# The w_down product of a gated MLP by seven instead of eight block products, with sums on GpSimd and VectorE, the keys' norms by a DMA of diagonals, and six instead of eight tiles for x

## The chip, the cores and the metric

The kernel runs on one core of a Trainium2 chip. A core has TensorE (matrix products, results to PSUM), VectorE, ScalarE and GpSimd (elementwise work; GpSimd does not read PSUM in this kernel) and SyncE, whose queue issues nearly all DMAs here. In the profile they are PE, with PEld for the loads of stationary operands, DVE, ACT, POOL and SP. The metric is the time of one execution on the device in microseconds; less is better. Before the change: 2123.92 us, median of 3 runs (2123.28 to 2125.16).

## The reference

32 sequences of 512 positions and 256 features, all in float32. Each goes through a delta-rule attention, an MLP and a gated MLP, each with layer norms and a residual sum:

```python
def delta(x, ...):
    q, k, v = split(x @ gates_w + gates_b, 3)
    lr = x @ lr_w + lr_b
    k = k / norm(k)
    A = tril(k k^T, -1) + I
    u = solve_triangular(A, v, lower=True)
    y = (q k^T) @ (lr * u)
    return y @ out_w + out_b

h = layernorm(x)
h = h + delta(layernorm(h) * dn_g + dn_b, ...)
h = h + relu((layernorm(h) * mn_g + mn_b) @ w1 + b1) @ w2 + b2
x = x + h
f = layernorm(x)
x = x + (silu(f @ wg.T) * (f @ wu.T)) @ wd.T   # wg, wu, wd: integers / 127; 768 hidden features
```

The last product of the last line is the one the change rewrites: for each sequence, a 512x768 matrix of hidden values times 768x256.

## The kernel before

Sequences are worked on in 16 pairs (`NS = 2`), one after another in a software pipeline written out by hand. In the loop at the end of the kernel, pass g handles three pairs together: `new` (keys, Gram matrix, triangular solve), `old` (MLP, gate and up products) and `older` (w_down product and output). In passes 2 to 15, that is 14 times, all three exist. The order of instructions on TensorE, VectorE, ScalarE and SP is the order of the code (`manual_schedule`); only GpSimd's order is chosen by the framework when the kernel is built, from which operations it expects to be ready.

A pass with all three pairs runs so:

1. `gram_phase`: Gram blocks of the new keys. `give` (L543) writes the 32x32 diagonal blocks of each Gram matrix to DRAM (`given`).
2. `middle` (L921): for the two old sequences `mlp_in`, `mlp_out` and `normed`, with the w_down products of the two older ones between them. `downs` (L873) yields eight steps, one for each sequence and chunk of 128 positions; `more(k)` takes the next k. A step (`Project.step`, L752) multiplies the 128 positions by all of w_down: six calls of 128x256 summed in PSUM. After every second step VectorE adds the 512 columns into the residual `s.acc` (L770); after the fourth, one DMA of 512 KB writes the sequence out (L871).
3. `gated` (L844): for each of the six blocks of 128 hidden features a gate product, `silu` on ScalarE, an up product, and their product on VectorE (L863). The results are six tiles of tag `hid`, twelve buffers in all. Twelve steps run before the solve of the new pair begins, and the other twelve are interleaved with it (`solution`, `solve`, `merge`).
4. `values_phase`: the rest of the attention of the new pair, and keys of the `following` pair.

Two more chains run on the side, as generators that a `Side` object advances whenever code on TensorE calls `spend` with the number of columns it has just used. `norms` (L555) multiplies each diagonal Gram block by the identity and sums it on VectorE, eight operations, then takes the power -- with exponent 0.5 -- on GpSimd; it is spread over 4*1024 columns. `invert` (L575) fetches `given` as `blocks`, inverts 64 triangular 32x32 blocks at once in 31 steps on VectorE (L603 a product, L607 a sum), writes the result to DRAM as `found` and reads it back as `yb` and `yfull`; it is paced by `INVERT`, 22*1024 columns. `merge` (L626) puts the 32x32 inverses together to 128x128 ones; it begins with VectorE transposes of `yb` (L636 to L638) and a TensorE product of them (L644).

In PSUM there are two pools of four banks; `mlp_in`, `mlp_out`, w_down, gate and up share `ps_f`. A bank comes free for the fourth tile after it when the engine that read it is done.

The residual, `s.a`, stays in one of eight 512 KB tiles of tag `a` from the load of x to the output. `load_a(following)` stands in `middle` ahead of the last five w_down steps. In `fetch_residual` (L806) GpSimd adds b2 to a second copy of x (L809). In `Norm.measure` GpSimd takes the power r_f or r_m (L345) and a product mr_f or mr_m (L373), which ScalarE's `apply` (L376) waits for.

Of the kernel before, what the change touches and what calls it, by code (L numbers as in the profile page):

```python
# [14 lines left out]
P = 128  # L15
# [6 lines left out]
def kernel(  # L22
# [98 lines left out]
    def big(name):  # L121
        return wk.tile([P, NT, C], F32, tag="a", name=name, bufs=8)
# [59 lines left out]
    class Gates:  # L182
# [63 lines left out]

        def turned(self, lo_, name):

            dst = wk.tile([P, NF, C], F32, tag="hid", name=name, bufs=NS * NH)
# [42 lines left out]
        def load_rest(self):  # L292
            self.load(*CUTS[1])
            self.load(*CUTS[2])
            self.ow = wk.tile([P, NF, C], F32, tag="hid", name="ow", bufs=NS * NH)
# [7 lines left out]
    wdT = const.tile([P, NH, C], F32, name="wdT")  # L303

    class Dequant:
        def __init__(self, src, name, tag, bufs):
            rows, self.cols = src.shape
            self.name, self.parts = name, []
            k = 1024 // self.cols
# [12 lines left out]
        def turn(self, dst):  # L322
            for r0, m, wi in self.parts:
                wf = wi.bitcast(F32)
                nc.scalar.mul(wf, wi, WSCALE)
                for cc in range(self.cols // P):
                    pt = ps_f.tile([P, 512], F32, tag="mm", name=f"{self.name}_t{cc}_{r0}")
                    for r in range(m):
                        nc.tensor.transpose(pt[:, ts(r, P)], wf[:, r, ts(cc, P)], ident)
                    nc.scalar.copy(dst[:, cc, r0 * P : (r0 + m) * P], pt[:, : m * P])  # L330
                    yield

# [57 lines left out]
    def to_features(src, dst, tag):  # L390

        for f in range(NF):
# [3 lines left out]
            nc.scalar.copy(grouped(dst[:, f, :]), natural(pt))  # L396
# [37 lines left out]
    def normalized(s):  # L434
# [41 lines left out]
        s.ag = wk.tile([P, NF, T], F32, tag="feat", name=f"ag_{n}", bufs=4)  # L476
# [24 lines left out]
    def to_keys(s):  # L501
        to_features(s.a, s.ag, f"a{s.n}")

    def keys(s, o):
        n = s.n
        if o == 0:
            s.kT = wk.tile([P, NF, T], F32, tag="ka", name=f"kT_{n}")

            early = n // NS == 1
            s.aT = wk.tile(  # L510
                [P, NF, T], F32, tag="a" if early else "aT", name=f"aT_{n}", bufs=8 if early else 2
            )
# [6 lines left out]
        nc.scalar.copy(natural(s.kT[:, o, :]), grouped(pk))  # L519
        nc.scalar.copy(natural(s.aT[:, o, :]), grouped(s.ag[:, o, :]))  # L520
# [22 lines left out]
    def give(s, given):  # L543
# [5 lines left out]
        for i in range(NB):  # L549
            rows = slice(i * B, (i + 1) * B)  # L550
            nc.sync.dma_start(
                given[:, i].rearrange("b r c -> r b c"), s.gd[rows, :, rows]
            )

    def norms(g, seqs):  # L555
        ss = small.tile([P, NS, NT], F32, tag="ss", name=f"ss_{g}", bufs=2)
        for slot, s in enumerate(seqs):
            for j in range(NT):
                junk = wk.tile([P, C], F32, tag="junk", name=f"js_{s.n}_{j}", bufs=1)
                nc.vector.tensor_tensor_reduce(  # L560
                    out=junk[:, :P], in0=s.gd[:, j, :], in1=ident, scale=1.0, scalar=0.0,
                    op0=ALU.mult, op1=ALU.add, accum_out=ss[:, slot, j : j + 1],
                )
                yield
# [4 lines left out]
        yield  # L569
# [5 lines left out]
    def invert(g, given, seqs):  # L575
# [5 lines left out]
            given.rearrange("s b i r c -> (s b i) (r c)").unsqueeze(1).to_broadcast(  # L581
# [262 lines left out]
    def gated(seqs):  # L844

        for s in seqs:
            s.hid = []
            for o in range(NH):
                g = wk.tile([P, T], F32, tag="hid", name=f"hid_{s.n}_{o}", bufs=NS * NH)
                s.hid.append(g)  # L850
# [15 lines left out]
    def down(s, c):  # L866
        if c == 0:
            s.project = Project(ps_f, s.acc, s.hid, wdT, NH, f"f{s.n}")
        s.project.step(c)
        if c == NT - 1:  # L870
            nc.sync.dma_start(out[s.n].rearrange("(c p) d -> p c d", p=P), s.acc)  # L871

    def downs(seqs):  # L873

        for s in seqs:
            for c in range(NT):
                down(s, c)
                yield
# [27 lines left out]
    def new_given(g):  # L906
        return dram.tile([NS, NT, NB, B, B], F32, tag="given", name=f"given_{g}")
# [13 lines left out]
    def middle(old, older, following):  # L921

        one, two = old
        rest = downs(older) if older else iter(())
        more = lambda k: [next(rest, None) for _ in range(k)]
        mlp_in(one, 0)
        mlp_in(one, 1)
        more(1)
# [5 lines left out]
        more(1)  # L934
        mlp_out(two, 0)
        mlp_out(two, 1)
        more(1)
# [246 lines left out]
```

## Time and profile before

The profiled execution took 2119.41 us, of which the span of instructions is 2117.5 us; the granted TensorE clock was 0.994 of full.

| engine | busy, us | share |
|---|---|---|
| loads of stationary operands | 1365.6 | 64% |
| VectorE | 1257.1 | 59% |
| ScalarE | 666.7 | 31% |
| GpSimd | 307.3 | 15% |

One pass, from the first `pa` of `middle` at 1143.96 us; rows of the windows view, busy time in each stretch:

```profile
core 0: us, PE busy (x) PEld busy (x) DVE busy (x) ACT busy (x) POOL busy (x), PEclk, DMA share, GB/s
1143.96:1162.90 18.94, 18.94 (x74) 13.68 (x73) 10.46 (x38) 6.17 (x16) 3.27 (x3) 1.00 0.25 69
1162.90:1178.45 15.55, 15.55 (x73) 13.68 (x72) 13.54 (x48) 2.08 (x4) 1.21 (x2) 1.00 0.53 131
1178.45:1199.06 20.61, 20.61 (x50) 9.12 (x49) 12.42 (x30) 3.59 (x6) 0.00 (x0) 1.00 0.38 106
1199.06:1243.00 43.94, 43.50 (x194) 28.03 (x193) 26.68 (x93) 14.32 (x42) 7.06 (x21) 1.00 0.24 72
```

Each row is a stretch: its bounds and length, then for each engine the busy time and the number of instructions, the granted clock, and what the DMA engines did. The first stretch is `middle` up to the last `mlp_out`, the second the last six w_down steps, the third the first twelve steps of `gated`, the fourth the solve and what follows.

A row of a group of instructions, elsewhere in this document, reads: line, engine, operation, output<-inputs, shapes, count | total busy us, mean ns of one | idle time of the engine before them, and what it waited for. A call of a float32 matmul in the code appears as two MATMUL rows of half the work each (w_down: 32 x 4 x 6 = 768 calls, 1536 rows), each with its own load. Matmuls overlap, so the mean of one is longer than the distance between two.

### The profile page before, as it was taken

The page shows a single profiled execution, that of the slowest core. Times are in us where ns is not written, and L with a number is a line of the kernel's source. Part 1 is how long each engine was busy: PE and PEld are TensorE (multiplying, and loading weights), DVE is VectorE, ACT ScalarE, POOL GpSimd, SP SyncE. Part 2 cuts the span into 40 slices and gives each one's busy share as a digit, 9 for nine tenths or more (in the row PEclk, how much of TensorE's full clock was granted, in tenths as well). Part 3 has the DMA queues.
Part 4 walks back from the last instruction along what each step waited for, and adds up shares of the span by engine and source line. Part 5 has one row for each costly group of instructions (what it writes and reads, how often), then busy time and mean ns, then how long its engine had stood idle before and what let it go on. Part 6 is the DMA issues. An engine that isn't in the chain of part 4 may idle for free.

```text
span 2117.5 us, 24970 instructions
## 1 busy us (share of the span) xinstructions
PE 2062.4 (97%) x7982; PEld 1365.6 (64%) x7982; DVE 1257.1 (59%) x4122; ACT 666.7 (31%) x1659; POOL 307.3 (15%) x551
## 2 busy tenths in 40 slices
PE   5799999999999999999999999999999999999999
PEld 2575666757666675766757566675766757566675
DVE  3747575765756566475765756566475755656331
ACT  3433313333142332323323242332323323241230
POOL 3101202112020211102111020211102011020100
PEclk9799999999999999999999999999999999999999
DMA  4110332413333222332413233231332422233020
GB/s 132 38 33 8 112 88 60 123 33 99 84 90 107 63 78 63 112 87 67 125 36 94 77 98 102 61 90 50 112 87 70 122 52 88 68 102 85 14 60 20
DMA packets 232459, 163.67 MB, mean 77 GB/s; under 512 B 64993, under 2 KB 207976, under 8 KB 232328
## 3 DMA queue, kind: packets, MB, share of 16 engines
q1 hardware_dynamic: 229136, 160.23, 27.0%
q10 hardware_dynamic: 3112, 1.71, 0.3%
q8 instruction: 64, 1.05, 0.2%
q14 instruction: 67, 0.55, 0.1%
q0 software_dynamic: 80, 0.14, 0.0%
HBM read 95.95 MB, written 66.06 MB: 77 GB/s over the span
## 4 chain that ended last, share of the span: by engine, by line
PE 83%; DVE 10%; ACT 4%; issue 1%; DMA 1%; POOL 0%; ACTq 0%; DVEq 0%; SPq 0%
PE po_f L758 16%; PE pup L854 13%; PE pgate L854 11%; PE pg L533 6%; PE po_d L758 5%; PE pf L719 5%; PE pa L824 5%; PE po_m L758 5%; PE pk L515 5%; PE pm L719 3%; PE pz L719 3%; ACT a L454 2%; PE pr L698 2%; DVE bnst_a L339 2%; PE pu L708 2%
## 5 line engine op out<-in xcount | busy, mean ns | idle before, releaser
L854 PE MATMUL pgate<-hT_f,wgT 128*128 128x512 f32 x768 | 364.3, 597 | 2.0 <-ACT hid L861 1.5
L854 PE MATMUL pup<-hT_f,wuT 128*128 128x512 f32 x768 | 364.0, 596 | 0.0
L758 PE MATMUL po_f<-wdT,hid 128*128 128x256 f32 x1536 | 339.2, 379 | 0.0
L758 PEld LDWEIGHTS po_f<-wdT,hid 128*128 128x128 f32 x1536 | 291.8, 190 | 52.9 <-issue 14.8
L861 ACT ACTIVATE hid<-pgate 128x512 f32<-128x512 f32 x192 | 114.3, 596 | 620.8 <-PE pgate L854 620.8
L863 DVE TENSOR_TENSOR hid<-hid,pup 128x512 f32<-128x512 f32 x192 | 131.0, 683 | 253.8 <-PE pup L854 252.5
L854 PEld LDWEIGHTS pgate<-hT_f,wgT 128*128 128x128 f32 x768 | 143.1, 190 | 146.7 <-issue 135.1
L854 PEld LDWEIGHTS pup<-hT_f,wuT 128*128 128x128 f32 x768 | 143.4, 190 | 145.8 <-issue 129.9
L607 DVE TENSOR_REDUCE xc<-xt 128x8 f32<-128x16 f32 (+30 forms) x496 | 147.0, 296 | 17.1
L603 DVE TENSOR_TENSOR xt<-xc,blocks 128x16 f32<-128x16 f32 (+30 forms) x496 | 147.3, 297 | 11.5
L533 PE MATMUL pg<-kT 128*128 128x256 f32 (+3 forms) x512 | 142.0, 434 | 0.6 <-ACT kT L519 0.6
L533 PEld LDWEIGHTS pg<-kT 128*128 128x128 f32 x512 | 89.8, 190 | 58.9 <-issue 35.6
L515 PE MATMUL pk<-ag,wa 128*128 128x512 f32 x256 | 119.2, 600 | 1.5 <-ACT ag L396 1.5
L758 PE MATMUL po_d<-m,aT 128*128 128x256 f32 x512 | 116.1, 380 | 1.1 <-ACT m L741 1.0
L758 PE MATMUL po_m<-w2s,act 128*128 128x256 f32 x512 | 116.3, 379 | 0.3
L719 PE MATMUL pf<-a,dp 128*128 128x256 f32 x512 | 115.6, 379 | 0.0
L824 PE MATMUL pa<-hT_m,w1s 128*128 128x512 f32 x256 | 115.1, 592 | 0.0
L758 PEld LDWEIGHTS po_d<-m,aT 128*128 128x128 f32 x512 | 96.8, 190 | 21.4 <-issue 3.6
L719 PEld LDWEIGHTS pf<-a,dp 128*128 128x128 f32 x512 | 97.3, 190 | 19.6 <-issue 7.2
L758 PEld LDWEIGHTS po_m<-w2s,act 128*128 128x128 f32 x512 | 97.1, 190 | 15.0 <-ACT act L830 1.5
L830 ACT ACTIVATE act<-pa,b1s 128x256 f32<-128x256 f32 x128 | 53.8, 471 | 157.0 <-PE pa L824 157.0
L742 DVE TENSOR_TENSOR m<-pm,obrow 128x256 f32<-128x256 f32 x32 | 13.6, 425 | 146.1 <-ACT m L741 146.1
(167 smaller groups left out, 2624.1 us busy)
## 6 DMA issues: line engine op xcount, KB each, us to landing
a<-in_L_attn_x_dram SPq DMA_DIRECT2D x32, 512.0 KB, 4.9
x<-in_L_attn_x_dram SPq DMA_DIRECT2D x32, 512.0 KB, 4.6
out_dram<-a SPq DMA_DIRECT2D x32, 512.0 KB, 3.6
way_m<-turn_m SPq DMA_DIRECT2D x120, 128.0 KB, 2.3
hT_m<-way_m SPq DMA_DIRECT2D x30, 512.0 KB, 3.7
way_a<-turn_a SPq DMA_DIRECT2D x112, 128.0 KB, 2.5
ag<-way_a SPq DMA_DIRECT2D x28, 512.0 KB, 6.9
way_f<-turn_f SPq DMA_DIRECT2D x112, 128.0 KB, 2.4
```

Of the source, the lines that this page charges most:

```text
L339: nc.vector.bn_stats(st[:, c, :], src[:, c, :])
L515: nc.tensor.matmul(pk, lhsT=wa[:, f, ts(o, P)], rhs=s.ag[:, f, :], start=(f == 0), stop=(f == NF - 1),)
L533: nc.tensor.matmul(pg[:, :w], lhsT=s.kT[:, f, ts(j, P)], rhs=s.kT[:, f, j * P :], start=(f == 0), stop=(f == NF - 1),)
L603: nc.vector.tensor_tensor(t[:, :, : i + 1], xc[:, :, : i + 1], blocks[:, i, : i + 1].unsqueeze(1).to_broadcast([P, ncol, i + 1]), ALU.mult,)
L607: nc.vector.tensor_reduce(xc[:, :, i], t[:, :, : i + 1], axis=AX.X, op=ALU.add)
L719: nc.tensor.matmul(s.pp[:, o, :], lhsT=lhs[:, c, ts(o, P)], rhs=rhs[:, c, :], start=(c == 0), stop=(c == nk - 1),)
L758: nc.tensor.matmul(self.po[:, c % 2, :], lhsT=src[:, ts(c, P)], rhs=self.w[:, f, :], start=(f == 0), stop=(f == self.nk - 1),)
L824: nc.tensor.matmul(pa, lhsT=w1s[:, f, ts(o, P)], rhs=s.hT[:, f, :], start=(f == 0), stop=(f == NF - 1),)
L830: nc.scalar.activation(natural(s.act[:, o, :])[:, :, some], grouped(pa)[:, :, some], AF.Relu, bias=b1s[:, o : o + 1], scale=1.0,)
L854: nc.tensor.matmul(pp, lhsT=w[:, f, ts(o, P)], rhs=s.hT[:, f, :], start=(f == 0), stop=(f == NF - 1),)
L861: nc.scalar.activation(natural(g), grouped(pp), AF.Silu)
L863: nc.vector.tensor_tensor(natural(g), natural(g), grouped(pp), ALU.mult)
```

## The change

**w_down.** The 512 positions of a sequence become two halves. In a half the hidden values are a 2x2 arrangement of blocks, A[i,k]: i picks one of two chunks of 128 positions, k the even or the odd of the six blocks of 128 hidden features. w_down is arranged likewise: k, and one of two blocks of 128 outputs. A product of two such 2x2 arrangements takes eight block products, or seven with sums of blocks before and after (the Strassen-Winograd scheme). Each block product is three calls of 128x128, since k runs over three pairs of features. `Down.plain` makes three products of unchanged blocks, then has GpSimd overwrite the four A blocks with their combinations; `Down.combined` makes the other four and adds everything into the residual, on VectorE and GpSimd, and then writes the half out (256 KB). The combinations of w_down are made once, in `Combined`.

```diff
-    wdT = const.tile([P, NH, C], F32, name="wdT")
+    NP = NH // 2
+    wdS = const.tile([P, NP, 7, P], F32, name="wdS")
...
+            if cc == NH - 1:
+                b = lambda i: wdS[:, :, i, :]
+                minus = lambda o, x, y: nc.gpsimd.tensor_tensor(o, x, y, ALU.subtract)
+                minus(b(5), self.b12, b(0))
+                minus(b(3), b(6), b(5))
+                minus(b(4), b(6), self.b12)
+                minus(b(2), b(1), b(3))
...
+        def products(self, po, todo):
+            for i, (block, slot) in enumerate(todo):
+                for j in range(NP):
+                    nc.tensor.matmul(
+                        po[:, i, :], lhsT=self.A[block][:, j, :], rhs=wdS[:, j, slot, :],
+                        start=(j == 0), stop=(j == NP - 1),
+                    )
+                spend(NP * P)
+        def plain(self):
+            name = f"{self.s.n}_{self.half}"
+            po = ps_f.tile([P, 4, P], F32, tag="mm", name=f"po_x_{name}")
+            self.products(po, [((0, 0), 0), ((0, 1), 1), ((1, 1), 2)])
+            self.e = wk.tile([P, P], F32, tag="e", name=f"e_{name}", bufs=4)
+            nc.scalar.copy(self.e, po[:, 0, :])
+            first = self.acc[:, :, :P]
+            nc.vector.tensor_tensor(first, first, po[:, 1:3, :], ALU.add)
+            A = self.A
+            nc.gpsimd.tensor_tensor(A[1, 0], A[1, 0], A[1, 1], ALU.add)
+            nc.gpsimd.tensor_tensor(A[0, 0], A[1, 0], A[0, 0], ALU.subtract)
+            nc.gpsimd.tensor_tensor(A[0, 1], A[0, 1], A[0, 0], ALU.subtract)
+            nc.gpsimd.tensor_tensor(A[1, 1], A[1, 1], A[0, 0], ALU.subtract)
+        def combined(self):
+            name = f"{self.s.n}_{self.half}"
+            po = ps_f.tile([P, 4, P], F32, tag="mm", name=f"po_y_{name}")
+            self.products(po, [((0, 0), 3), ((1, 1), 4), ((1, 0), 5), ((0, 1), 6)])
+            w = wk.tile([P, 3, P], F32, tag="uv", name=f"uv_{name}", bufs=1)
+            acc, flat = self.acc, self.acc.rearrange("p c d -> p (c d)")
+            twice = lambda m: m.unsqueeze(1).to_broadcast([P, 2, P])
+            add = lambda o, x, y: nc.vector.tensor_tensor(o, x, y, ALU.add)
+            add(w[:, 0, :], self.e, po[:, 0, :])
+            add(w[:, 1:3, :], twice(w[:, 0, :]), twice(po[:, 1, :]))
+            add(acc[:, :, P:], acc[:, :, P:], twice(po[:, 2, :]))
+            add(acc[:, 0, P:], acc[:, 0, P:], po[:, 3, :])
+            nc.gpsimd.tensor_tensor(acc[:, 0, :P], acc[:, 0, :P], self.e, ALU.add)
+            nc.gpsimd.tensor_tensor(
+                flat[:, P:], flat[:, P:], w.rearrange("p b d -> p (b d)"), ALU.add
+            )
+            nc.sync.dma_start(
...
     def downs(seqs):
...
+        return [Down(s, h) for s in seqs for h in range(NT // 2)]
```

**The order in `middle`** (and likewise, in other places, in `last_middle` and after the last `gated`); the load of the following pair moves from here to the seventh step of `gated`:

```diff
         mlp_in(one, 1)
-        more(1)
+        for d in rest[:1]:
+            d.plain()
...
         normed(one, "f")
-        more(1)
+        for d in rest[1:2]:
+            d.plain()
         mlp_out(two, 0)
         mlp_out(two, 1)
-        more(1)
         turned(one, "f")
+        for d in rest[:1]:
+            d.combined()
         normed(two, "f")
-        if following:
-            for s in following:
-                load_a(s)
-        more(5)
+        for d in rest[2:]:
+            d.plain()
+        for d in rest[1:]:
+            d.combined()
```

**Norms.** The row of `given` is made 32 elements longer, so that a stride of 33 over it walks all diagonals; one DMA of 1024 single elements replaces the eight VectorE operations. The side chain is spread over 16*1024 columns.

```diff
-    def norms(g, seqs):
+    def norms(g, given, seqs):
         ss = small.tile([P, NS, NT], F32, tag="ss", name=f"ss_{g}", bufs=2)
-        for slot, s in enumerate(seqs):
-            for j in range(NT):
...
-                yield
+        nc.sync.dma_start(
+            ss.rearrange("p s t -> p (s t)"),
+            given.rearrange("s b i e -> (s b) (i e)")[:, :: B + 1].rearrange("q t -> t q"),
+        )
+        yield 4
...
-                kn_side = Side(norms(g, new), 10, 4 * 1024)
+                kn_side = Side(norms(g, given, new), 10, 16 * 1024)
```

**Room.** Tag `a` has six buffers instead of eight; `hid` becomes one tile of six blocks for each sequence, two buffers, which also hold weights at the start. For the first four sequences the keys' input is kept in natural order and one ScalarE copy for each half of the features goes away:

```diff
-        return wk.tile([P, NT, C], F32, tag="a", name=name, bufs=8)
+        return wk.tile([P, NT, C], F32, tag="a", name=name, bufs=6)
...
-        nc.scalar.copy(natural(s.kT[:, o, :]), grouped(pk))
-        nc.scalar.copy(natural(s.aT[:, o, :]), grouped(s.ag[:, o, :]))
+        if n >= 2 * NS:
+            nc.scalar.copy(natural(s.kT[:, o, :]), grouped(pk))
+            nc.scalar.copy(natural(s.aT[:, o, :]), grouped(s.ag[:, o, :]))
+        else:
+            nc.scalar.copy(s.kT[:, o, :], pk)
...
-            s.hid = []
+            s.hid = wk.tile([P, NH, T], F32, tag="hid", name=f"hid_{s.n}")
```

## Prediction

> **What bounds the kernel now.** I read the page's busy times first, then the chain that ended last, then the groups of instructions with shapes kept apart, then one steady stage in order of time, engine by engine.
>
> ```profile
> PE 2062.4 (97%) x7982; PEld 1365.6 (64%) x7982; DVE 1257.1 (59%) x4122; ACT 666.7 (31%) x1659; POOL 307.3 (15%) x551
> ...
> PE 83%; DVE 10%; ACT 4%; issue 1%; DMA 1%; POOL 0%; ACTq 0%; DVEq 0%; SPq 0%
> ...
> L758 PE MATMUL po_f<-wdT,hid 128*128 128x256 f32 x1536 | 339.2, 379 | 0.0
> ```
>
> TensorE is busy 97% of the span and is most of the chain; the w_down products are its third largest group. Shares over the span hide what happens within a stage, so here is one of the 14 stages that have a pair in the solve, a pair in the MLP and an older pair in w_down (TensorE, then VectorE and the DMA queue):
>
> ```profile
> 1143.96 3.60 PE L824 MATMUL pa<-hT_m,w1s 128*128 128x512 f32 x8
> ...
> 1162.91 15.70 PE L758 MATMUL po_f<-wdT,hid 128*128 128x256 f32 x72
> 1178.45 1.88 PE L854 MATMUL pgate<-hT_f,wgT 128*128 128x512 f32 x4
> ```
> ```profile
> 1155.52 0.35 DVE L589 RECIPROCAL di<-blocks 128x32 f32<-128x32 f32 x1
> ...
> 1175.38 0.29 DVE L603 TENSOR_TENSOR xt<-xc,blocks 128x136 f32<-128x136 f32 x1
> 1175.71 0.30 DVE L607 TENSOR_REDUCE xc<-xt 128x8 f32<-128x136 f32 x1
> ...
> 1190.08 0.42 DVE L607 TENSOR_REDUCE xc<-xt 128x8 f32<-128x256 f32 x1
> ```
> ```profile
> 1190.53 0.34 SPq L611 DMA_DIRECT2D found<-xc  x1
> 1192.25 0.91 SPq L618 DMA_DIRECT2D yb<-found  x2
> ```
>
> I count from 1143.96 as t=0. TensorE has no gap up to t=56. But from t=11.6 to t=46.5 VectorE is full too, but for some 2 us: the 31 steps of the inversion, a product and a sum each, fill the gaps between its other work and end at t=46.5. `found` and `yb` follow (issue at 48.3, 0.9 us, 2.0 us to landing: 4.6 us in all), and the merge, whose first transpose of `yb` ran at t=56.0, needs them. So there is a second chain, VectorE's, about 5 us behind the first. 59% busy does not show it.
>
> **The change, part by part.** *TensorE.* Each product of the code is two instructions (768 calls, 1536 rows). A stage has 96 of 128x256; 15.54 us for 72 in a row (the chain's piece) is 0.216 each: 20.7 us. It gets 2 sequences x 2 halves x 21 calls x 2 = 168 of 128x128. The nearest row is the last Gram block:
>
> ```profile
> 128.79 0.61 PE L533 MATMUL pg<-kT 128*128 128x128 f32 x4
> ```
>
> Its single duration is 274 ns, so (0.61-0.27)/3 = 0.113 from start to start; eight transposes of that width give (1.04-0.27)/7 = 0.110. 168 x 0.111 = 18.6 us: **2.1 us less a stage**, 34 us in all. A rule speaks against this: the Trainium skill, "TensorE: Matmul & The Clock Gate", § Back-to-back issue gap, says weight load and matmul together set the spacing of a narrow stream, and has 81 ns where its formula for the matmul alone has 56. That ratio on 0.111 makes 0.160: 27 us a stage, 6 us more instead of 2.1 less. The row is nearer: same type, same widths, a load per matmul (190 ns, overlapping the next). It runs in fours, though, and the new runs are 18 and 24 long; I take 0.111 and keep the rule as a rival.
>
> *GpSimd.* It gets 16 sums of 128x384 a stage, and 8 smaller ones into the output.
>
> ```profile
> L809 POOL TENSOR_TENSOR x<-x,b2s 128x1024 f32<-128x1024 f32 x32 | 74.7, 2356 | 34.3 <-DMA x<-in_L_attn_x_dram 32.3 <-PE pu L708 1.9
> ...
> L373 POOL TENSOR_TENSOR mr_m<-nmn_m,r_m 128x4 f32<-128x4 f32 x32 | 6.4, 200 | 2.5
> ```
>
> From these, 0.2 + 2.1 ns an element: 1.0 us for 384, 0.47 for 128. A dependent pair (r_m, then mr_m) has a gap of 0.08, so the four sums of a half take **4.2 us**. On average that hides. It doesn't where it bunches. In the new order the last three-product groups end at t=22.4 and 24.4, and their four-product groups are to start at 27.1 and 29.8. From 22.4 GpSimd has r_f and mr_f of the second sequence (1.3 us, released by VectorE about then), eight sums (8.5), and perhaps the two additions of the first group (1.4): the last sum is ready at 32.2 or 33.6. The last group wants it for its second product at 30.4. TensorE waits 1.8 to 3.2 us; bounds 0.5 (sums first, faster than the row) and 4. I take **2.6**.
>
> *VectorE.* A half had one 128x512 addition, 0.60 from start to start. It gets one of 256 columns after its first group and after the second 128, 256, 256, 128, two of them dependent. At about 1 ns a column (683 against 425 ns for 512 and 256) that is 0.36 + 1.38. Inside the full stretch fall three of the first kind and four of the second: 6.6 us for 2.4, **4.2 more**. It starts 1.2 us earlier (two groups of 2.6 us ahead of it become 2.0), and 1.0 us of waiting for ScalarE's `h_f` is filled. The inversion ends at 48.5 instead of 46.5. The norms' removal (8 rows of 0.37 us) frees time at t=-4 to 1, outside the stretch, where VectorE then idles until the first po_m at t=8: nothing.
>
> Then there is what the two engines share:
>
> ```profile
> 1156.11 1.23 DVE L592 TENSOR_TENSOR blocks<-blocks,ndi 128x1024 f32<-128x1024 f32 x1
> ```
> ```profile
> 1156.77 0.63 POOL L373 TENSOR_TENSOR mr_f<-nmn_f,r_f 128x4 f32<-128x4 f32 x1
> ```
> ```profile
> 1961.21 1.49 DVE L640 TENSOR_SCALAR rhs<-a,kn 128x256 f32<-128x256 f32 x1
> ```
>
> A 0.20 us GpSimd operation took 0.63 and ended 0.06 after VectorE's product of two SBUF operands. And a 0.35 us VectorE operation took 1.49 while a 2.35 us GpSimd addition ran beside it. The Trainium skill, "SBUF — State Buffer", § Who interferes with whom, makes it a rule: a VectorE instruction with two SBUF inputs and a GpSimd one that reads SBUF exclude each other, whole instruction against whole instruction. Every inversion step begins with such a product. But `xt` rows beside the short powers r_f kept their 250 ns, so the trace does not show this pair colliding. With the rule, some 8 steps among the sums lose 0.4 us each, 3.2 us (up to 6 with the additions): the inversion ends at 51.7; without it, at 48.5. The sums stream their operands as the 1024-wide addition does, so I go with the rule. At 51.7, `yb` lands at 56.3 and the merge's first product comes at 57.6 instead of 56.9; TensorE would have been there at 57.4 by the lines above, and the second sequence's transposes follow as late. Lateness also shows in PSUM: w_down, gate and up share four buffers, so the second `up` waits when the last group's four additions end over 5 us after its matmuls. For both I take **0.9 us**; bounds 0 and 2.7.
>
> *ScalarE* gets 4 copies of 128x128 a stage (266 ns); it is idle 9 us before the gates. *Norms by DMA*: one issue (about 0.5 us) ahead of `blocks` on SP, 1024 pieces of 4 bytes. Bounds for `blocks` 0.5 us (the issue) and 6 us (landing of b1s, 256 such pieces, in the crowded start); it lands near 8 and is wanted at 11, so 0; at worst 2.7 us of VectorE. The power waits for it on GpSimd with r_f behind, but is 6,554 columns late by its schedule, about 11 us. *Six tiles*: the next x can load only when an older output has left. On SP the outputs now wait for GpSimd's last addition (t≈42), with `hT_f` of the second sequence (wanted at t=55) and both loads behind: in by about t=52, wanted at 68. Free; without that cover each us late is one on the path.
>
> *Ends.* At the start ScalarE loses eight copies (620 ns) and VectorE 3 us of norms before the first inversion; TensorE waits there for both: -2. In the last middle, 10.4 us of products covering the m round trip become 6.7 and wait for sums: that eats its 2.1. The tail saves 2.1 and adds about 1.2 of small additions: -1.
>
> **Sum.** -2.1 + 2.6 + 0.9 = +1.4 a stage, x14 = +20, ends -3: span 2117.5 + 17 = 2134.5, execution 2119.41 + 17 = 2136. The median of the runs lies 4.5 above the profiled execution, so **2140**.
>
> **Rivals.** *The sums hide*: GpSimd takes eight sums before anything else and the exclusion hardly bites; -2.1 to -0.5, say -1.3 a stage: -18-3, 2103 (all of it kept: 2092). For it: POOL is idle 85% of the time, and its order is chosen by readiness, not by the code (the x addition ran after a later copy). Against: 8.5 us of dependent sums in 8 us. *Full exclusion*: 6 us on the inversion and 4 at the sums; +3.3, 2167. Slower, decided at t=46.5 to 49: once the last reduction ends beyond about 50 the merge moves out. *Narrow products pay for their loads*: 0.160 each, +6 a stage, 2220; against it the rows of 0.11. *A part that doesn't do what it says* (norms late, x late): 3 in 100.
>
> **Chances.** Mine 0.41 (own range 2122 to 2158), sums hide 0.38, full exclusion 0.15, loads 0.03, other 0.03. Range **2092 to 2172**: from the full saving to full exclusion. A difference of 0.2% (4 us) is what can be told from none. Of mine 0.06 and of the hidden sums 0.02 fall within it, and 0.01 of the rest: faster 0.37, same 0.09, slower 0.54.
>
> **What would show it.** The new products 0.111 apart, in runs of 18 and 24; sums of about 1.0 us; waits of the four-product groups on GpSimd, 2 to 3 us a stage; `xt` rows beside a sum longer than before; the last reduction at 50 to 53 after the first `pa`. I'm wrong if no product waits for GpSimd, if `xt` keeps its length, or if the spacing nears 0.16.

## The result and the profile after

The changed kernel takes **2115.79 us** (median of 6 runs, 2114.84 to 2116.86) against 2123.80 us (6 runs, 2123.28 to 2125.16): ratio 0.9961, 95% interval 0.9948 to 0.9974. It is faster by 0.4%; the prediction had 0.8% slower as the likeliest. The result lies inside its outer range (2092 to 2172), but not inside its own (2122 to 2158), and on the other side of the kernel before.

The profiled execution took 2116.25 us, its span 2114.5. First the page: busy times, chain of waits, groups.

```profile
PE 2037.7 (96%) x9134; PEld 1373.7 (65%) x9134; DVE 1351.0 (64%) x4122; ACT 673.9 (32%) x1714; POOL 663.9 (31%) x939
...
PE 66%; DVE 19%; ACT 5%; issue 3%; POOL 3%; DMA 2%; ACTq 0%; SPq 0%; POOLq 0%; DVEq 0%
...
L645 DVE TENSOR_TENSOR xt<-xc,blocks 128x16 f32<-128x16 f32 (+30 forms) x496 | 200.4, 404 | 9.1
L925 PE MATMUL po_y<-wdS,hid 128*128 128x128 f32 x1536 | 179.8, 276 | 9.1 <-DVE a L938 9.1
...
L649 DVE TENSOR_REDUCE xc<-xt 128x8 f32<-128x16 f32 (+30 forms) x496 | 147.0, 296 | 17.1
```

TensorE lost 25 us of busy time, VectorE gained 94, and its share of the chain went from 10% to 19%. All new idle time in front of the four-product groups is put down to VectorE (L938, the addition behind a three-product group), none to GpSimd. The inversion's products take 404 ns on average; its sums (L649) keep their 296. Before:

```profile
L603 DVE TENSOR_TENSOR xt<-xc,blocks 128x16 f32<-128x16 f32 (+30 forms) x496 | 147.3, 297 | 11.5
```

One pass, from the first `pa` at 1142.66 us, on TensorE:

```profile
1160.45 2.84 PE L925 MATMUL po_y<-wdS,hid 128*128 128x128 f32 x24
1163.13 4.18 PE L925 MATMUL po_x<-wdS,hid 128*128 128x128 f32 x36
1167.15 5.52 PE L925 MATMUL po_y<-wdS,hid 128*128 128x128 f32 x48
1173.32 2.92 PE L925 MATMUL po_y<-wdS,hid 128*128 128x128 f32 x24 [0.65 <-DVE a L938]
...
1183.63 1.98 PE L895 MATMUL pgate<-hT_f,wgT 128*128 128x512 f32 x4 [0.52 <-DVE a L953]
```

Less one duration of 0.276, 24 products stand (2.84 - 0.276)/23 = 0.1115 apart. So a pass, where 168 narrow products stand for 96 wide ones, saves 96 x 0.216 - 168 x 0.1115 = 2.0 us. In brackets are the two waits, both for an addition that has to read a PSUM bank before it comes free. GpSimd and VectorE in the same pass:

```profile
1164.05 1.00 POOL L942 TENSOR_TENSOR hid<-hid 128x384 f32<-128x384 f32 x1 [2.84 <-PE po_x L925]
1165.12 1.00 POOL L943 TENSOR_TENSOR hid<-hid 128x384 f32<-128x384 f32 x1
1166.08 1.00 POOL L944 TENSOR_TENSOR hid<-hid 128x384 f32<-128x384 f32 x1
1167.04 1.02 POOL L381 TENSOR_TENSOR r_f<-ve_f,neghalf 128x4 f32<-128x4 f32 x1
...
1170.33 1.01 POOL L944 TENSOR_TENSOR hid<-hid 128x384 f32<-128x384 f32 x1
...
1198.50 2.00 POOL L941 TENSOR_TENSOR hid<-hid 128x384 f32<-128x384 f32 x2 [13.82 <-DVE hid L904]
```
```profile
1165.16 1.03 DVE L645 TENSOR_TENSOR xt<-xc,blocks 128x64 f32<-128x64 f32 x1
...
1171.63 0.76 DVE L614 TENSOR_TENSOR kn<-kn,r 128x4 f32<-128x4 f32 x2
...
1193.90 0.42 DVE L649 TENSOR_REDUCE xc<-xt 128x8 f32<-128x256 f32 x1
```

Behind a three-product group stand three sums, not four. The fourth (L941, `A[1,0] += A[1,1]`) runs a pass earlier, as soon as the hidden values are there: the two at 1198.50 are for the next pass. And the row of the last two groups begins at 1164.05, t=21.4, right behind the first product of its group (six of the 36 rows from 1163.13, through at about 1163.96); it does not wait for the other two (about 1165.3). The last sum ends at 1171.3, t=28.7; the product that reads it would come at about 30.7. An inversion product of 128x64 that takes 0.22 us alone took 1.03 beside a sum, and the last reduction ends at 1194.3, t=51.7, in every full pass (46.5 before).

Where the spans differ, stretch by stretch:

| stretch | before, us | after, us | difference |
|---|---|---|---|
| to the first `pa` of all | 146.24 | 145.96 | -0.3 |
| first distance between passes | 112.12 | 112.24 | +0.1 |
| 13 distances between full passes | 126.51 each | 126.21 in ten, 127.18 in three | -1.0 |
| last full pass to `pa` of `last_middle` | 121.82 | 118.35 | -3.5 |
| from there to the end | 92.65 | 94.24 | +1.6 |
| span | 2117.5 | 2114.5 | -3.0 |

The fourth and fifth rows belong together: `last_middle` now has 60 narrow products (6.7 us) ahead of that `pa` where it had 48 wide ones (10.4), and the rest behind it. Of the 8.0 us between the medians the two profiled spans show 3. The kernel before was quicker in its profiled executions than in most others (2119.41, and 2120.08 in a second one; the others on record lie between 2118.97 and 2128.0); the changed one was not. What those 5 us are no trace shows.

The three long passes differ at the merge. One of them, VectorE (the pass begins at 763.0):

```profile
818.12 0.69 DVE L904 TENSOR_TENSOR hid<-hid,pup 128x512 f32<-128x512 f32 x1 [2.23 <-PE pup L895]
819.30 0.30 DVE L678 STREAM_TRANSPOSE xparts<-yb 32x128 f32<-32x128 f32 x1 [0.50 <-DMA yb<-found]
...
820.26 0.72 DVE L682 TENSOR_SCALAR rhs<-a,kn 128x256 f32<-128x256 f32 x1
```

Here `yb` lands at about t=56.2 and VectorE waits 0.50 us for it; in the other passes it lands at about 55.4 and the first transpose follows `hid` at once, at t=55.7. Before the change it landed at 50.3. So the slack of the second chain is used up: a transpose that comes 0.2 to 0.6 us late, as in these three passes, costs 1 us, since `rhs` then also meets GpSimd's early sums (0.72 us here, else 0.35). What delays the landing in these passes isn't known.

### The profile page after: what moved, and what is told of

Its sections match the earlier page's. It is cut to its first block, busy times and chain, and to the rows that moved or that the text cites. A ratio compares the mean times of both kernels' runs of the same rounds, so it can differ in the third digit from the quotient of the medians.

```text
span 2114.5 us, 27772 instructions
## 1 busy us (share of the span) xinstructions
PE 2037.7 (96%) x9134; PEld 1373.7 (65%) x9134; DVE 1351.0 (64%) x4122; ACT 673.9 (32%) x1714; POOL 663.9 (31%) x939
## 4 chain that ended last, share of the span: by engine, by line
PE 66%; DVE 19%; ACT 5%; issue 3%; POOL 3%; DMA 2%; ACTq 0%; SPq 0%; POOLq 0%; DVEq 0%
PE pup L895 10%; PE pgate L895 7%; PE pg L577 6%; PE pf L761 5%; PE po_m L800 5%; PE pa L866 5%; PE po_d L800 5%; PE pk L556 5%; DVE xt L645 4%; PE po_x L925 3%; DVE xc L649 3%; PE pz L761 3%; PE pm L761 3%; ACT a L493 2%; PE pr L740 2%
## 5 line engine op out<-in xcount | busy, mean ns | idle before, releaser
L645 DVE TENSOR_TENSOR xt<-xc,blocks 128x16 f32<-128x16 f32 (+30 forms) x496 | 200.4, 404 | 9.1
L925 PE MATMUL po_y<-wdS,hid 128*128 128x128 f32 x1536 | 179.8, 276 | 9.1 <-DVE a L938 9.1
L925 PEld LDWEIGHTS po_y<-wdS,hid 128*128 128x128 f32 x1536 | 176.1, 192 | 12.0 <-issue 11.3
L941 POOL TENSOR_TENSOR hid<-hid 128x384 f32<-128x384 f32 x64 | 67.1, 1069 | 366.0 <-DVE hid L904 366.0
L649 DVE TENSOR_REDUCE xc<-xt 128x8 f32<-128x16 f32 (+30 forms) x496 | 147.0, 296 | 17.1
L925 PEld LDWEIGHTS po_x<-wdS,hid 128*128 128x128 f32 x1152 | 135.1, 192 | 15.8 <-issue 15.5
L942 POOL TENSOR_TENSOR hid<-hid 128x384 f32<-128x384 f32 x64 | 64.1, 1001 | 242.2 <-PE po_x L925 242.2
L925 PE MATMUL po_x<-wdS,hid 128*128 128x128 f32 x1152 | 136.4, 275 | 0.0
L938 DVE TENSOR_TENSOR a<-a,po_x 128x256 f32<-128x256 f32 x64 | 26.3, 413 | 155.9 <-ACT e L936 155.9
```

Of the source, the lines that this page charges most:

```text
L645: nc.vector.tensor_tensor(t[:, :, : i + 1], xc[:, :, : i + 1], blocks[:, i, : i + 1].unsqueeze(1).to_broadcast([P, ncol, i + 1]), ALU.mult,)
L649: nc.vector.tensor_reduce(xc[:, :, i], t[:, :, : i + 1], axis=AX.X, op=ALU.add)
L925: nc.tensor.matmul(po[:, i, :], lhsT=self.A[block][:, j, :], rhs=wdS[:, j, slot, :], start=(j == 0), stop=(j == NP - 1),)
L941: nc.gpsimd.tensor_tensor(A[1, 0], A[1, 0], A[1, 1], ALU.add)
```

## The experiments

The theory going in: TensorE saves 2.0 us a pass; GpSimd's sums are in time, but they hold up VectorE, and through PSUM banks and the merge VectorE gives nearly all of it back. All but before_again and before_late_load start from the changed kernel; where the edit shown is against another run, it says so.

**no_sums.**

```diff
-            nc.gpsimd.tensor_tensor(A[1, 0], A[1, 0], A[1, 1], ALU.add)
-            nc.gpsimd.tensor_tensor(A[0, 0], A[1, 0], A[0, 0], ALU.subtract)
-            nc.gpsimd.tensor_tensor(A[0, 1], A[0, 1], A[0, 0], ALU.subtract)
-            nc.gpsimd.tensor_tensor(A[1, 1], A[1, 1], A[0, 0], ALU.subtract)
```


> Leaves out the four GpSimd sums of hidden blocks in each half (64 halves), so the second set of products works on unsummed blocks. Theory (TensorE saves 2.0 us a pass; most of it is given back because GpSimd's sums hold up VectorE's inversion and additions, and through PSUM banks TensorE): the products of the inversion fall from a mean of 0.404 us to 0.30 to 0.33, the inversion's last reduction from 51.7 us after the pass begins to 47 to 49, the two waits of TensorE for VectorE (0.65 and 0.52 us) to under half of that, no pass is longer by 1 us at the merge, and the whole goes to 2092 to 2103 us. Rival (VectorE's own additions, 4.2 us a pass, are the cause): the last reduction stays at 50 or later, both waits stay, 2111 to 2116 us. Rival (TensorE waits for the sums themselves): faster too, but by waits of the second products on GpSimd that the trace of the changed kernel would have to show.

2090.05 us, 2 us below the range expected; ratio 0.9848 (0.9832 to 0.9865). A pass takes 124.61 us, the last reduction ends at t=48.1, and neither wait of TensorE is left: the last three groups run as one.

```profile
1151.33 8.20 PE L925 MATMUL po_y<-wdS,hid 128*128 128x128 f32 x72
```
```profile
L645 DVE TENSOR_TENSOR xt<-xc,blocks 128x16 f32<-128x16 f32 (+30 forms) x496 | 161.0, 325 | 9.1
```

VectorE's additions are all still there, so alone they cost 124.61 - (126.51 - 2.0) = 0.1 us a pass. That rival is out. The third, that TensorE waits for the sums themselves, is ruled out by the changed kernel's own trace, in which no product waits for GpSimd. The norms by transfer are still there too: without the sums they cost no more than that 0.1 either.

**memsets** asks what about the sums holds VectorE up.

```diff
-            nc.gpsimd.tensor_tensor(A[1, 0], A[1, 0], A[1, 1], ALU.add)
+            nc.gpsimd.memset(A[1, 0], 0.5)
...
```


> The changed kernel with each GpSimd sum of hidden blocks replaced by a GpSimd write of a constant to the same block, at the same place (other values, sums left out). Theory (a sum holds up VectorE because it reads the on-chip memory while VectorE's product reads two operands): the writes do not, the inversion's products fall to a mean of 0.29 to 0.33 us as without sums, 2088 to 2097 us. Rival (any GpSimd access, or GpSimd being busy at all, slows VectorE): the mean stays above 0.35 us and the time above 2100 us.

2088.92 us (2 runs), ratio 0.9835 (0.9813 to 0.9857). The groups view:

```profile
L645 DVE TENSOR_TENSOR xt<-xc,blocks 128x16 f32<-128x16 f32 (+30 forms) x496 | 160.6, 324 | 9.0
...
L942 POOL MEMSET hid<- 128x384 f32 x64 | 26.7, 417 | 266.4 <-PE po_x L925 266.4
```

The writes are shorter than the sums (0.42 against 1.00 us), but 64 x 4 of them leave `xt` at 324 ns, the value without any sums (325). Nor is it that the writes miss the products: of the 16 products of 128x64, 14 run beside a write and take 0.22 us, as alone, where beside a sum 14 took 1.03 to 1.05. Writing doesn't hold VectorE up; a sum that reads does. (The last reduction ends at t=49.5 here, 1.4 us later than in no_sums; the passes are as short, 124.55 us.)

**first_sum_behind** makes the first sum, too, wait for the first products, as the prediction had assumed.

```diff
+            nc.gpsimd.tensor_copy(A[1, 0][:, 0, 0:1], self.e[:, 0:1])
             nc.gpsimd.tensor_tensor(A[1, 0], A[1, 0], A[1, 1], ALU.add)
```


> Before the first GpSimd sum of each half, one column of the block it overwrites is replaced by a column of the first product (changed values there), so that this sum, too, has to wait for the first products, as the prediction had taken it: four dependent sums follow each set of first products, not three. Prediction's account: the second half's last sum comes 1 to 2 us later, the third half's about 3 us later (two more sums and two copies ahead of it), TensorE waits for GpSimd 1 to 3 us a pass, and the whole is at 2125 to 2150 us. Rival (the sums hide even so, because TensorE comes to the second products late anyway): within 5 us of the changed kernel, 2111 to 2121 us.

2189.05 us, ratio 1.0315 (1.0299 to 1.033): slower than both. TensorE in one pass (it begins at 1171.3):

```profile
1200.47 0.94 PE L925 MATMUL po_y<-wdS,hid 128*128 128x128 f32 x6 [1.81 <-POOL hid L943]
1203.42 6.38 PE L925 MATMUL po_y<-wdS,hid 128*128 128x128 f32 x42 [2.02 <-POOL hid L945]
```

The wait of the prediction appears, on the engine it named: 3.8 us a pass where it had 2.6 (bounds 0.5 to 4). Over the whole run TensorE waits 61.0 us for sums. But the run doesn't show what the first sums alone would cost, for two reasons. GpSimd's order, chosen anew, moved more than them:

```profile
1194.07 1.02 POOL L381 TENSOR_TENSOR r_f<-ve_f,neghalf 128x4 f32<-128x4 f32 x1 [2.43 <-DVE nmn_f L407]
...
1196.91 1.00 POOL L960 TENSOR_TENSOR a<-a,uv 128x384 f32<-128x384 f32 x1 [1.54 <-DVE a L954]
...
1198.30 0.99 POOL L942 TENSOR_TENSOR hid<-hid 128x384 f32<-128x384 f32 x1
```

r_f, mr_f and an addition to the output now stand ahead of the third half's sums, which begin at t=27.0, with GpSimd idle for 4.0 us on the way; and the sums of the third and fourth half come in turns, so the third half's last sum is the fifth of that row. (An estimate for two more sums in the changed kernel's own row, from 1.00 us and a gap of up to 0.08 each: it would end at t=30.8 instead of 28.7, about when its product would come, 30.7. So they alone might hardly have made TensorE wait.)

And waiting isn't all that it lost. A row of the windows view, right behind the second wait:

```profile
1203.00:1206.40 3.40, 2.98 (x14) 2.98 (x15) 3.23 (x9) 0.00 (x0) 3.40 (x5) 0.51 0.02 5
```

The granted clock is 0.51 there. In all 14 full passes it falls like this after these waits, for 3.4 or 6.8 us, where in the changed kernel's passes, with waits of 0.65 and 0.52 us, it stays at 1.00. The 42 products take 6.38 us here and 7.71 in other passes; 0.1115 apart they would take 4.8. That is 1.5 or 2.9 us of a pass, and makes the difference between the passes of 130.3 and those of 131.7. Without it a pass would be about 128.8, still longer than the 126.5 before.

**norms_back** undoes the transfer of diagonals alone.

```diff
-        nc.sync.dma_start(
-            ss.rearrange("p s t -> p (s t)"),
-            given.rearrange("s b i e -> (s b) (i e)")[:, :: B + 1].rearrange("q t -> t q"),
-        )
...
+                nc.vector.tensor_tensor_reduce(
+                    out=junk[:, :P], in0=s.gd[:, j, :], in1=ident, scale=1.0, scalar=0.0,
+                    op0=ALU.mult, op1=ALU.add, accum_out=ss[:, slot, j : j + 1],
+                )
...
-                kn_side = Side(norms(g, given, new), 10, 16 * 1024)
+                kn_side = Side(norms(g, given, new), 10, 4 * 1024)
```


> The changed kernel with the keys' norms on VectorE again (eight products with the identity, 3.0 us a pass, right after the Gram blocks). Theory: VectorE has room in the first 16 us of a pass (8.4 busy), the work there ends before the crowded stretch begins, so 0 to 0.5 us a pass: 2115 to 2123 us. Rival (the gain of the change comes from the norms): 2122 us or more, with the inversion's last reduction at 53 or later.

2105.97 us, ratio 0.9923 (0.9909 to 0.9938): 10 us *faster* than the changed kernel, a pass 125.30 us. Neither side had expected that: the new way to take the norms costs time. Of TensorE's two waits the first is gone (the second is 0.49 us):

```profile
1164.33 8.20 PE L927 MATMUL po_y<-wdS,hid 128*128 128x128 f32 x72
```

Two things move with the reductions. The power on GpSimd (1.63 us), which in the changed kernel stands ahead of the second half's sums, stands ahead of all sums here; and two multiplications of 128x4 on VectorE come at t=6 instead of t=29, where a GpSimd addition to the output (L959) stretches them from 0.23 us for both to 0.76. Three runs take that apart.

**norms_back_late** (edit against norms_back)

```diff
+        yield 8
         kn = small.tile([P, NS, NT], F32, tag="kn", name=f"kn_{g}", bufs=2)
         nc.gpsimd.tensor_tensor(
             kn.rearrange("p s t -> p (s t)"), ss.rearrange("p s t -> p (s t)"), half, ALU.pow
         )
-        yield
+        yield 16
```


> As norms_back (reductions on VectorE at the start of the pass), but the power on GpSimd and the two multiplications on VectorE that end the norms are held back to where the changed kernel has them: the power behind the first r_f, the multiplications in the crowded stretch. Theory (norms_back gained 0.9 us a pass because the power, 1.63 us, no longer stands ahead of the second half's sums and the two multiplications, 0.76 us, no longer stand in the crowded stretch): the gain goes, a pass is 126.0 to 126.4 us, the whole 2114 to 2120 us. Rival (the transfer of the diagonals itself, ahead of the transfer of the blocks, was the cost): a pass stays at 125.3 us and the whole at 2104 to 2108 us.

2115.47 us, ratio 0.996 (0.9945 to 0.9975), a pass 126.08: the gain is gone with no transfer in it, so it is the place that costs. But GpSimd's order is chosen when the kernel is built, and the power stayed ahead of all sums; only the multiplications were late.

**mults_late** (edit against norms_back)

```diff
-        yield
+        yield 24
         for slot, s in enumerate(seqs):
             s.kn = kn[:, slot, :]
```


> As norms_back, the power on GpSimd early as there, and only the two multiplications on VectorE held back to the crowded stretch. If the multiplications in that stretch are what the changed kernel's norms cost (0.76 us of VectorE, where it is full), a pass is 125.9 to 126.2 us and the whole 2112 to 2117 us. If it is the power of 1.63 us on GpSimd ahead of the second half's sums, which pushes those sums onto more steps of the inversion, a pass stays at 125.3 to 125.5 us and the whole at 2104 to 2109 us.

2116.83 us, ratio 0.9959 (0.9945 to 0.9974), a pass 126.07. As the run before, in effect: the multiplications in the crowded stretch cost 0.8 us a pass.

**mults_at_end** goes the other way, from the changed kernel.

```diff
-        yield 4
+        yield 24
         for slot, s in enumerate(seqs):
             s.kn = kn[:, slot, :]
```


> The changed kernel with all norms by transfer as it has them, and one number changed: the two multiplications on VectorE that end the norms (0.76 us for both in the crowded stretch) are held back until the inversion's last step is through, where VectorE waits 2 us for the up products anyway. Theory (these two multiplications are what the norms cost, and the transfer costs nothing): a pass of 125.2 to 125.6 us and 2100 to 2106 us with the early start of the changed kernel. Rival (the power on GpSimd ahead of the second half's sums, or the transfer, counts as well): 2107 to 2114 us.

2124.89 us, ratio 1.0005 (0.9996 to 1.0013): both expectations missed, in the other direction. A pass takes 127.02 us, 0.95 of it at the merge. VectorE there:

```profile
1203.71 0.23 DVE L614 TENSOR_TENSOR kn<-kn,r 128x4 f32<-128x4 f32 x2
...
1204.81 1.16 DVE L682 TENSOR_SCALAR rhs<-a,kn 128x256 f32<-128x256 f32 x1
```

The two short rows push `rhs` into GpSimd's early sums (1203.87, 1.95 us for two), and the second product of the merge waits 1.23 us instead of 0.28. Without that the pass would be about 126.07: taking the multiplications out of the stretch brought no more than 0.1, since the power was still late. What each version has, in us after the pass begins:

| version | power ahead of second half's sums | multiplications in the stretch | second inversion step takes | third half's L938 starts | pass |
|---|---|---|---|---|---|
| norms_back | no | no | 0.18 | 29.00 | 125.30 |
| mults_late | no | yes | 0.18 | 29.96 | 126.07 |
| mults_at_end | yes | no | 0.72 | 29.95 | 127.02, 0.95 of it at the merge |
| changed kernel | yes | yes | 0.72 | 30.11 | 126.21 |

Either cause makes VectorE about 1 us late at the third half's addition, and both together hardly more. In all four GpSimd is busy without a gap from t=21.4 to t=29.6 (six sums, r_f, mr_f, one addition). A VectorE that is late goes through that row beside other sums, and what it loses is set by where they end. So far the trace; that reading wasn't tested by itself.

**early_inv**

```diff
-        yield 14 * B
+        yield 8 * B
...
-            yield B + i
+            yield 0.6 * (B + i) if 2 * i <= B else 1.4 * (B + i)
+        yield 2 * B + B
```


> The changed kernel with another pace of the inversion and nothing else: it begins about 4 us earlier, its first 16 steps come closer together and the later ones further apart, and the write of the result is ordered at the same place as before. Theory (TensorE loses about 1.7 us a pass to VectorE being full, 16.2 of 17.1 us, between 16 and 33 us of the pass): the stretch has fewer or less crowded steps, the last reduction ends at 46 to 50 us, the three long passes become normal, the waits of 0.65 and 0.52 shrink, 2100 to 2112 us. Rival (the pace of the inversion isn't what makes VectorE late, the additions behind the products are): 2114 to 2118 us.

2171.57 us, ratio 1.023 (1.0215 to 1.0245): a miss by 60 us. The earlier steps got in front of the layer norm's statistics on VectorE, and the newly built order of GpSimd has r_f of the first sequence behind the second half's sums, at t=16.2 instead of 11.1. TensorE waits 1.40, 0.97, 1.67 and 0.21 us a pass, always for VectorE. Two things moved, so the run doesn't say what the pace alone would do.

**before_late_load** tests the later load of x alone, in the kernel before.

```diff
-        if following:
-            for s in following:
-                load_a(s)
         more(5)
...
+                    if i == 6 and following:
+                        for s in following:
+                            load_a(s)
```


> The kernel before with one part of the six tiles alone: the load of the following pair's x moves from the middle of the pass to behind the seventh step of the gate and up products; the eight tiles stay. Theory (the load is hidden in both places): a pass of 126.5 us, within 3 us of before. Rival (the later load is part of the gain, since it no longer meets the traffic of the inversion): 2 us or more below before and a shorter pass.

2122.88 us (12 runs), ratio 1.0001 (0.999 to 1.0012), passes of 126.51 us: nothing, as expected. (In its profile the way to `last_middle` is 3.6 us longer: at one merge TensorE waits 2.39 us for VectorE instead of 0.37, and the granted clock is 0.59 in the 4.2 us from 1963.0, behind it.) The count of tiles itself wasn't tried alone.

**before_again**

> The kernel before once more, for a second profile: if its profiled execution was a quick one, the span is now 2120 to 2123 us with the passes still at 126.5 us, the rest outside them; if not, 2117 to 2118 us as before.

2120.08 us, span 2118.2, every full pass 126.51 to 126.53, the last reduction at 46.5: between the two cases named. The passes are the same from run to run, so the differences of tenths above can be read; ahead of the first `pa` executions of like kernels differ by about 1.5 us.

**first_norms_only** puts together what was learned: the transfer where it gains, at the start, and VectorE's reductions in the passes.

```diff
+        norms_ = first_norms(0, given, first)
...
-                kn_side = Side(norms(g, given, new), 10, 16 * 1024)
+                kn_side = Side(norms(g, given, new), 10, 4 * 1024)
```


> The changed kernel with the norms by transfer for the first pair alone and on VectorE for the other fifteen. Theory: the later passes are those of norms_back (125.3 us), and the first pass starts 3 us earlier than there, as in the changed kernel (146.0 against 149.1): 2100 to 2105 us, faster than both kernels. Rival (the 3 us at the start are chance): 2105 to 2108 us.

2103.04 us, ratio 0.9901 (0.9884 to 0.9917). Most passes are 125.3 us, and the first `pa` comes at 146.2 us, against 148.3 to 149.1 in the three versions of the changed kernel that have all norms on VectorE. (The kernel before, with all norms on VectorE, has it at 146.2 as well, so something else in the change costs 2 to 3 us at the start. What, no run shows.)

**two_uv** goes after the tail, where VectorE waits for the one buffer that it shares with GpSimd (edit against first_norms_only). In the changed kernel:

```profile
2103.80 0.29 DVE L953 TENSOR_TENSOR uv<-e,po_y 128x128 f32<-128x128 f32 x1 [2.31 <-POOL a L959]
```
```diff
-            w = wk.tile([P, 3, P], F32, tag="uv", name=f"uv_{name}", bufs=1)
+            w = wk.tile([P, 3, P], F32, tag="uv", name=f"uv_{name}", bufs=2)
```


> first_norms_only with two buffers instead of one for uv, the sums that VectorE hands to GpSimd in the last addition of a half. In the tail VectorE waits 4.5 us for GpSimd to be done with the one buffer (2.29, 1.11 and 1.10 us before the last three halves), while the passes show no such wait. Theory: the passes keep 125.3 us, and from the last pa of the last middle to the end it gets 1 to 3 us shorter (94.3 us now), as the tail then ends one GpSimd addition behind the last product: 2099 to 2103 us. Rival (GpSimd's own row of sums sets the tail): no difference, 2102 to 2105 us.

2101.15 us, ratio 0.9892 (0.9876 to 0.9909). The waits are gone and the tail is 93.6 us instead of 94.3: 0.7, less than expected, as the end follows the last product. In the profiled execution the first `pa` also came 1.3 us earlier, so only the 0.7 is shown. Of the versions that leave nothing out this is the fastest.

## Why the prediction was wrong

The step that failed, in its words: "From 22.4 GpSimd has r_f and mr_f of the second sequence (1.3 us, released by VectorE about then), eight sums (8.5), and perhaps the two additions of the first group", hence "I take **2.6**" us a pass of waiting for sums. It read the code's order as GpSimd's and let all four sums of a half wait for the whole three-product group, so that the last sum was ready at 32.2 or 33.6. In the changed kernel it is ready at 28.7, and the wait is 0. Two of the eight sums aren't in the row: the first sum of a half touches only `A[1,0]`, which no first product reads, and adds `A[1,1]` without changing it; nothing but the hidden values holds it back, and it ran in the pass before. That is 2.1 us. And the row begins at 21.4, not 22.4, since its first sum waits for one product, the one that reads the block it overwrites: 1.0 us. The small rest is sums that follow more closely. first_sum_behind shows that sums behind the products can make TensorE wait, and that the kernel is then slower; as its order on GpSimd differs in more than that, it gives neither part its size.

By its other steps:

- *TensorE, -2.1*: right. 0.1115 us apart in runs of 18 and 24; 2.0 saved. The higher spacing for narrow products in the Trainium skill, "TensorE: Matmul & The Clock Gate", § Back-to-back issue gap, which the prediction set aside, has no counterpart here.
- *Sums of 1.0 us, 0.08 between dependent ones*: right (1.00 us, starts 0.96 to 1.08 apart).
- *The exclusion of two-operand products on VectorE and reads on GpSimd* (the Trainium skill, "SBUF — State Buffer", § Who interferes with whom): right. "The inversion ends at 51.7" with the rule: 51.7, to the tenth by luck, as it is 48.1 without the sums (48.5 predicted) and they add 3.5 (3.2 predicted). The inversion's products take (200.4 - 147.3) / 14 = 3.8 us a pass more than before, 2.8 of it by the sums (161.0 without them).
- *+0.9 for VectorE's lateness*: right in kind, too small, and in part at other places. It is 126.21 - (126.51 - 2.0) = 1.7 in most passes, 2.7 in the three long ones, 1.9 on average. The merge was to be 0.7 late in every pass, with `yb` at 56.3; `yb` lands at 55.4, and three passes are late. The waits for PSUM banks stand at the last four-product group (0.65) and at a gate product (0.52), not at the second `up`. By the runs: 0.1 VectorE's additions, 0.7 the sums (norms_back against no_sums), 0.9 the norms' end in the stretch (changed kernel against norms_back), the rest at the merge. The 0.9 exists only beside the sums: no_sums has the same norms.
- *Norms by transfer, 0*: wrong. The transfer was hidden as it said, but the two last multiplications and the power, which move with it, weren't priced where they land. Having the transfer in the passes, and not at the start alone, costs 2115.79 - 2103.04 = 12.7 us.
- *Six tiles, 0*: no sign of a cost; the load's part was shown free.
- *Ends, -3*: -0.3 at the start, -1.9 for `last_middle` and the tail together, no wait for sums in `last_middle`: -2.0 with the first distance. The single `uv` buffer took 0.7 of it.

So 2.6 was put in that isn't there, 1.0 left out that is, and 0.1 too much taken for TensorE's saving: 1.5 us a pass too slow, 20 us over 13 passes. The other 4 us of the miss are the distance between profiled execution and median, which was carried over from the kernel before; the changed kernel's profiled execution lies at its median. Of the rivals, "the sums hide" was right about GpSimd and wrong about the exclusion; the truth was a mixture that no case had.

## What to carry to other kernels

When an engine's order is made by readiness, read each operation's operands before counting it into a row: in a chain of in-place sums the first may be free long before the rest, and each of the others waits only for the product that reads the block it overwrites. A run that is to test one dependence on such an engine needs a look at the whole order it got. Sums moved to an idle GpSimd are paid on VectorE wherever it multiplies two operands from the on-chip memory at that time, so place them against VectorE's full stretch, not against GpSimd's share of the span. And when a step changes its unit, follow its small tail: two operations of 128x4 that landed in a full stretch cost 0.8 us a pass (mults_late against norms_back), while the 3 us of reductions that the change took away had stood where VectorE was not full.

## What the hardware showed

How long a GpSimd sum stretches a VectorE instruction that starts beside it depends on what that one reads. From the changed kernel's trace, medians by the output and inputs of the instruction: alone, and where it starts inside a GpSimd instruction of over 0.4 us:

| VectorE instruction | reads | alone, us | beside |
|---|---|---|---|
| `xt<-xc,blocks` | two tiles in SBUF | 0.32 | 0.66 |
| `kn<-kn,r`, 4 columns | two tiles in SBUF | 0.15 | 0.68 |
| `a<-a,po_y` | SBUF and PSUM | 0.35 | 0.35 |
| `turn_f<-h_f`, transpose | one tile | 0.45 | 0.45 |
| `xc<-xt`, sum over columns | one tile | 0.33 | 0.25 |

(The last row is shorter beside the sums since the smaller steps fall there.) So the additions that read PSUM, which the change adds to VectorE, pass GpSimd unhindered, and those that fetch both operands from SBUF wait, however few columns they have. An instruction with one tile can wait as well. The prediction showed such a row (`rhs`, 1.49 us instead of 0.35), but counted the cost of the sums on products of two operands alone. Here is one with four columns, in norms_back, where a sum runs from 1161.22 to 1162.21:

```profile
1161.46 0.78 DVE L403 TENSOR_SCALAR ve_f<-bnmv_f 128x4 f32<-128x4 f32 x1
```

It takes 0.17 us alone. The Trainium skill, "SBUF — State Buffer", § Who interferes with whom, lists `tensor_scalar` among those that can take the shared ports when their operands meet certain conditions. Whether these operands meet them no run here shows; transposes and sums over columns, which read one tile too, kept their length.

The second thing is the granted clock of TensorE. Two waits of 1.81 and 2.02 us with 0.94 us of products between them were followed by a clock of 0.5 for 3.4 or 6.8 us in every full pass of first_sum_behind, and by 1.5 or 2.9 us of lost time; waits of 0.65 and 0.52 us, 10 us apart, left it at 1.00 in the changed kernel. So a wait of TensorE can cost more than its length.
